# Weight sums in the first eight steps of gate and up, and the first output tile prepared from slot 114 of attention on

## The chip, the cores and the metric

The kernel runs on one core of a Trainium2 chip. The metric is the device time of one execution in microseconds (us); 2352.47 is the median of three runs before the change (2349.41 to 2353.89). Engines: PE is TensorE (matmuls; PEld its weight loads), DVE is VectorE, ACT is ScalarE, POOL is GpSimd, SP is SyncE, which here issues every DMA in one queue, in order.

## The reference

The reference is one transformer block on 4096 tokens of 512 features: linear attention with 16 query heads on 4 key heads, a residual and a layer norm, then a feed-forward part whose inputs go through a Hadamard transform, a second residual and a layer norm.

```python
q, k, v = x @ Wq.T, x @ Wk.T, x @ Wv.T            # 16, 4 and 4 heads of 128
q, k = rope(q), rope(k)
qf, kf = elu(q) + 1, elu(k) + 1
state_t = state_(t-1) + kf_t (outer) v_t;  z_t = z_(t-1) + kf_t
out_t = (qf_t @ state_t) / (qf_t . z_t + 1e-6)
x = layernorm(x + out @ Wo.T)
h = fwht(x * SU_ug) / 64
h = silu(h @ W_gate.T * (Wscale * 64)) * (h @ W_up.T * (Wscale * 64))
h = fwht(h * SU_dp) / 64
x = layernorm(x + h @ W_down.T * (Wscale_dp * 64))
```

## The kernel before

Every matmul operand is split into a high and a low part (`hilo`, lines 92 to 94: a copy on ACT, then a subtraction on DVE or POOL), and each product is three matmuls (high x high, high x low, low x high).

**Attention.** Tokens come in 16 blocks of 256, and the loop runs over them twice, once for key heads 0 and 1 and once for 2 and 3: 32 blocks n of four slots (g, p), 128 slots i, `NQ = 128`. A slot projects a pair of query heads (`proj_q`, L279), makes scores (`scores`, L372 and L373, then the sum of their halves on DVE, L382 and L383, and a causal mask on POOL, L386) and applies them (`av`, L406 and L407). `av` writes the numerators to `num_d` and the denominators to `den_d` in DRAM, for each tile t of 128 tokens. `recip(b)` (L123) loads the denominators of a block, inverts them and writes `rec_d`; it is called for a block of the second pass after its last slot, one block later (L571).

Beside this the loop loads and splits the second pass's weights (slots 54 to 58), splits the 16 heads of Wo and puts both parts into `wo_d` (`wo_stage`, at slots 112 to 116), loads them back as the storage of used weights comes free (`wo_fetch`), and forms weight sums for gate and up (`wcomb`, in blocks 18 to 25). `wcomb(p)` loads four quarter matrices A11, A12, A21, A22 from `wug` and makes S3 = A11 - A21, S1 = A21 + A22, S2 = S3 - A22, S4 = A12 + S2 on POOL (L429), each put into `was_d`.

A scheduler orders the instructions of each engine, so the place in the source is not the place in the queue: it may pull such side work many slots forward. In the order of the built kernel the sums stand in blocks 14 to 19, and the Wo splits in blocks 19 to 22.

**Output projection.** 32 tiles t. `pre(t)` loads the numerators (`nt`, 1 MB) and the residual (`yp`); `pre_rb` loads a row of reciprocals, spread over all partitions (`rb`, 256 KB, one for each key head g). `norm_o` (L708) multiplies them (g even on DVE, L713; g odd on POOL, L716) and splits the product; `wo_tile` (L157) runs 48 matmuls a tile into `ps_wo`. The first tile is made at the end of attention (lines 574 to 585, `ps_w0`): its `pre(0)` stands at slot 124, where the storage of the attention's inputs (`early`) is closed and that of `late["p"]` opens in its place. Layer norm, the transforms (`front`) and the preparation of the down weights (`prep_down`) run beside it.

**Gate and up.** 32 steps n = (f, p): 4 stretches of tokens by 8 pairs of weight tiles, each a product of two by two blocks in seven multiplications (Winograd's form; SEQ, WKEY). In step n, `asplit(n + 1, s)` splits the operands of the next step, and `aload(n + 2, s, ...)` loads those of the one after: three or four from `wug`, the sums from `was_d`, into `rp` (10 buffers). The results of a step are multiplied and summed on POOL (L900, L978) and put into `hop_d` one step later (`late_puts`).

**Down projection.** 56 units of 48 matmuls (L1041), with the second residual and layer norm; it isn't touched.

Of the kernel before, what the change touches and what calls it, by code (L numbers as in the profile page):

```python
# [9 lines left out]
F32 = mybir.dt.float32  # L10
# [33 lines left out]
def kernel(  # L44
# [8 lines left out]
    def dma(dst, src, pin=False):  # L53
        if dst.dtype == F32R:
            dst = dst.bitcast(F32)
        if src.dtype == F32R:
            src = src.bitcast(F32)
        i = nc.sync.dma_start(dst, src)  # L58
        if pin:
            tc.keep_in_program_order(i)  # L60
# [46 lines left out]
        dma(wo_d[h][0], hi)  # L107
        dma(wo_d[h][1], lo)

    def wo_fetch(h0, h1):  # L110
        for h in range(h0, h1):
            if h < NH - 2:
                hi, lo = (wres.tile([128, 512], F32R, tag="w", name=x) for x in ("wh", "wl"))
            else:
                w = late["p"].tile([128, 2, 512], F32R, tag="wx", name="wx")
                hi, lo = w[:, 0], w[:, 1]
            dma(hi, wo_d[h][0])
            dma(lo, wo_d[h][1])
            WO.append((hi, lo))

    late = {}

    def recip(b):  # L123
        dn = pout.tile([128, 2, 16], F32, tag="dn", name="dn", bufs=2)
        for j in range(2):
            dma(dn[:, j], den_d[2 * b + j].rearrange("g h c q -> (g h c q)").rearrange("(p n) -> p n", p=128))
        V.reciprocal(dn, dn)
        for j in range(2):
            dma(rec_d[2 * b + j].rearrange("(p n) -> p n", p=128), dn[:, j])

    cur = {}

    def pre_rb(t, g, pin=False):
        rb = late["p"].tile([128, 512], F32, tag="rb", name="rb", bufs=4)
        dma(rb, rec_d[t][g * 512:(g + 1) * 512].partition_broadcast(128), pin)
        cur[t]["rb"].append(rb)

    def pre(t):
        if t in (12, 16):
            recip(NB - 2 + (t == 16))  # L140
        nt = late["p"].tile([128, 16, 128], F32, tag="nt", name="nt", bufs=2)
        cur[t] = dict(nt=nt, rb=[])
        if t:
            dma(nt, num_d[t].rearrange("p g n -> p (g n)"), t < 3)
        if t < 2:
            for g in range(4):
                if t == 0:
                    dma(nt[:, 4 * g:4 * g + 4], num_d[t][:, g])
                pre_rb(t, g, t == 1 and g == 0)
        if t % 2 == 0:  # L150
            k = t // 2 % 3
            cur["yp"] = (late["c2"].tile([128, 2, DM], F32, tag="yp", name="yp", bufs=1) if k == 2 else
                         late["p"].tile([128, 2, DM], F32, tag="yp", name="yp", bufs=2))
        cur[t]["yp"] = cur["yp"]
        dma(cur["yp"][:, t % 2], x_n[t * 128:(t + 1) * 128])

    def wo_tile(t, ps, after=None):  # L157
        i = 0
        for g in range(KVH):
            oh, ol = cur[t][g]  # L160
            for h in range(4):
                wh, wl = WO[4 * g + h]
                for l, r in ((oh, wh), (oh, wl), (ol, wh)):
                    T.matmul(ps, l[:, h], r, start=i == 0, stop=i == 47)  # L164
                    i += 1
            if after is not None:
                after(g)


    with ExitStack() as es:  # L170
# [246 lines left out]
                    dma(den_d[2 * b + j][gg].rearrange("h c q -> c h q"),  # L417
                        ds[2 * j:2 * j + 2].rearrange("c (h q) -> c h q", h=4))

        def wcomb(p):  # L420
            r = {}
            for it in range(2):
                for kh in range(2):
                    x = wres.tile([128, 2, 2, 128], F32, tag="w", name="wq")
                    dma(x, wug[2 * p + it].rearrange("p (u k m) -> p u k m", u=2, k=4)[:, :, 2 * kh:2 * kh + 2])
                    r[it, kh] = x
            for key, o, a, b, op in (("S3", (0, 0), (0, 0), (1, 0), ALU.subtract), ("S1", (1, 0), (1, 0), (1, 1), ALU.add),
                                     ("S2", (1, 1), (0, 0), (1, 1), ALU.subtract), ("S4", (0, 1), (0, 1), (1, 1), ALU.add)):
                G.tensor_tensor(r[o], r[a], r[b], op)  # L429
                dma(was_d[p][key], r[o].rearrange("p u k m -> p (u k m)"))  # L430

        N = 2 * NB
        slots = [(n, g, p) for n in range(N) for g in range(2) for p in range(2)]
# [58 lines left out]
        for i, (n, g, p) in enumerate(slots):  # L492
# [8 lines left out]
                weights_q(1, 0)  # L501
            if r == 3 - QA:
                weights_q(1, 1)
            if 4 * 28 <= i < 4 * 28 + 4:
                for h in range(3 * (i - 112), 3 * (i - 112) + 3):
                    wo_stage(h)
            if i == 4 * 29:
                for h in range(12, 16):
                    wo_stage(h)
            if i == NQ - 10:  # L510
                wo_fetch(0, 2)
            if i == NQ - 6:
                wo_fetch(2, 6)
            if i == NQ - 5:
                wo_fetch(6, 10)
            if i == NQ - 4:
                wo_fetch(10, 14)
                early.close()
                late["s"] = ExitStack()
                late["p"] = late["s"].enter_context(tc.tile_pool(name="cl", bufs=2, side="right", reuse_waits="tile"))  # L520
                pre(0)
                wo_fetch(14, 16)
            go(gq)
            if sl == (0, 1):
                go(gk)
            if sl == (1, 0):
                go(gk)
            gq2 = proj_q(i + QA) if i + QA < NQ else None
            go(gq2)
            if sl == (0, 0):  # L530
# [33 lines left out]
            for x in gsc:  # L564
                go(x)
            gq = gq2
            if sl == (1, 0) and 18 <= n < 26:
                wcomb(n - 18)
            if sl == (1, 1):
                if NB + LAG <= n < N - 2 + LAG:  # L570
                    recip(n - NB - LAG)  # L571
                blk.pop(n - 1, None)

        pre(1)
        for x in range(2):
            o2 = [p3.tile([128, 2, 4, 128], F32R, tag=t, name=t, bufs=4) for t in ("qh", "ql")]
            for y in range(2):
                g = 2 * x + y
                rb = cur[0]["rb"][g].rearrange("p (h n) -> p h n", h=4)
                (G if y else V).tensor_tensor(rb, cur[0]["nt"][:, 4 * g:4 * g + 4], rb, ALU.mult)  # L580
                hilo(o2[0][:, y], o2[1][:, y], rb)
                cur[0][g] = (o2[0][:, y], o2[1][:, y])
        ps0 = pmm.tile([128, DM], F32, tag="mm", name="ps_w0")
        wo_tile(0, ps0)
        V.tensor_tensor(cur[0]["yp"][:, 0], ps0, cur[0]["yp"][:, 0], ALU.add)
# [100 lines left out]

    def aload(n, s, x):
        p, key = n % 8, WKEY[s]
        if key[0] == "A":
            it, kh = 2 * p + (key[1] == "2"), key[2] == "2"  # L690
            dma(x, wug[it].rearrange("p (u k m) -> p u k m", u=2, k=4)[:, :, 2 * kh:2 * kh + 2])
        else:
            dma(x, was_d[p][key].rearrange("p (u k m) -> p u k m", u=2, k=2))
        RAW[n, s] = x

    def asplit(n, s):
        hi, lo = (wres.tile([128, 2, 2, 128], F32R, tag="w", name=x) for x in ("woh", "wol"))
# [4 lines left out]
    with ExitStack() as es:  # L702
# [4 lines left out]

        def norm_o(t, g):  # L708
            c = cur[t]
            rb = c["rb"][g].rearrange("p (h n) -> p h n", h=4)  # L710
            if g % 2 == 0:
                o32 = pon.tile([128, 4, 128], F32, tag="on", name="ps_on")
                V.tensor_tensor(o32, c["nt"][:, 4 * g:4 * g + 4], rb, ALU.mult)  # L713
            else:
                o32 = p2.tile([128, 4, 128], F32, tag="o32", name="o32")
                G.tensor_tensor(o32, c["nt"][:, 4 * g:4 * g + 4], rb, ALU.mult)  # L716
            hi, lo = (p2.tile([128, 4, 128], F32R, tag="o", name=n, bufs=8) for n in ("oh", "ol"))
            hilo(hi, lo, o32)
            c[g] = (hi, lo)
# [65 lines left out]
        for t in range(32):  # L785
            if t + 2 < 32:
                pre(t + 2)
            def after(g):
                if t == 31:
                    for s in (2 * g, 2 * g + 1):  # L790
                        if s < 7:
                            asplit(0, s)
                if t + 1 < 32:
                    norm_o(t + 1, g)
                    if t + 2 < 32:
                        pre_rb(t + 2, g)

            yp = cur[t]["yp"]
            if t:
# [67 lines left out]
    with ExitStack() as es:  # L867
# [23 lines left out]
        for n in range(NS):  # L891
# [3 lines left out]
            def emit(u, q, x):  # L895
# [3 lines left out]
                else:  # L899
                    G.tensor_tensor(x, x, c.pop(("g", q)), ALU.mult)  # L900
                    c["h", q] = x

            if n in (1, 2, 4, 5):
                step(fr, 9)
                fr = ff_front(12 + (1, 2, 4, 5).index(n))
            new = {}
            for s, tag in enumerate(SEQ):
# [3 lines left out]
                for u in (1, 0):  # L911
# [20 lines left out]
                    if s == 5:  # L932
                        if u == 1:
                            x = utile("sg")
                            S.activation(x, ps, AF.Silu, scale=sc)
                            c["g", 2] = x
                        else:
                            x = c.pop(("g", 2))
                            V.scalar_tensor_tensor(x, ps, sc, x, ALU.mult, ALU.mult)
                            c["h", 2] = x  # L940
                if n and s in (1, 2, 3):
                    for _ in range(3):
                        if late_puts:
                            late_puts.pop(0)()
# [175 lines left out]
```

## Time and profile before

| what | us |
|---|---|
| median of three runs | 2352.47 |
| the profiled execution | 2353.87 |
| its span, first to last instruction | 2352.2 |
| attention, up to the first ps_wo | 0 to 976.1 |
| output projection | 976.1 to 1366.7 |
| gate and up | 1366.7 to about 2010 |
| down projection | about 2011.7 to 2352.2 |

The mean granted clock of TensorE was 0.990. PE was busy for 97% of the span, but a busy PE counts the overlap of pipelined matmuls, so a stage is judged by the idle time between them and by the time that a block, tile or step takes. The DMA queue moved 500.94 MB, 213 GB/s on average, with stretches above 280.

In the profile's rows a group of instructions is given as line, engine, operation, output <- inputs, shapes, count, then busy us and mean ns, then the idle time of that engine just before and what ended it. A row of waits gives who waited for whom, us in total, how often, and the longest. The chain of waits is followed back from the last instruction: start us, length, what.

### The profile page before, as it was taken

The numbers are of one execution on the slowest core, as the hardware profiler recorded it, in microseconds if no ns is written. First come the engines' busy times: TensorE is split into PE (matmuls) and PEld (weight loads), VectorE is DVE, ScalarE is ACT, GpSimd is POOL, SyncE is SP. The second block draws the span as 40 slices with busy tenths as digits, with TensorE's granted clock in tenths as the row PEclk, the third lists the DMA queues.
The fourth block names the chain that finished last, engine by engine and source line by source line (L and its number), as shares of the span: only waits on it lengthen the run. The fifth ranks groups of instructions, "written<-read, shape, count | busy, mean of one in ns | idle before, by whom it ended". The sixth has DMA issues, their size and how long they took to land.

```text
span 2352.2 us, 42395 instructions
## 1 busy us (share of the span) xinstructions
PE 2272.5 (97%) x14432; PEld 2013.3 (86%) x14432; DVE 1804.5 (77%) x2794; ACT 1401.9 (60%) x2482; POOL 1256.5 (53%) x1005
## 2 busy tenths in 40 slices
PE   8999999998899999899999999999999999899998
PEld 8999999887889999688878777788878888799998
DVE  8999999888898888578888775676776766665555
ACT  7777777766677777344434365655655655555553
POOL 4545544567655444358776626565565556633332
PEclk9999999999999999899999999999999999999999
DMA  6555555676785446879889976775665756877673
GB/s 205 169 162 147 148 149 153 192 223 202 236 268 147 134 139 201 286 252 284 250 277 271 280 255 196 246 252 188 225 210 188 243 188 197 265 248 249 225 250 118
DMA packets 378744, 500.94 MB, mean 213 GB/s; under 512 B 69694, under 2 KB 225408, under 8 KB 374560
## 3 DMA queue, kind: packets, MB, share of 16 engines
q1 hardware_dynamic: 378528, 498.24, 68.0%
q8 instruction: 114, 1.87, 0.3%
q14 instruction: 102, 0.84, 0.1%
HBM read 291.15 MB, written 165.15 MB: 194 GB/s over the span
## 4 chain that ended last, share of the span: by engine, by line
PE 74%; DVE 9%; DMA 7%; issue 4%; POOL 3%; ACT 2%; SPq 1%; DVEq 0%; ACTq 0%; POOLq 0%
PE ps_a L918 14%; PE ps_wo L164 13%; PE ps_qk L279 11%; PE ps_da L1041 7%; PE ps_b L918 7%; PE ps_num L406 4%; PE ps_db L1041 4%; PE ps_c L918 4%; PE ps_s L329 3%; PE ps_v L232 2%; PE ps_dc L1041 2%; DMA rb<-rec_d 1%; DVE x L265 1%; SPq L58 1%; PE ps_sc L372 1%
## 5 line engine op out<-in xcount | busy, mean ns | idle before, releaser
L386 POOL TENSOR_SCALAR_AFFINE_SELECT A<-A 64x512 fp32r<-64x512 f32 x256 | 224.6, 878 | 294.1 <-DVE am L382 195.7
L279 PE MATMUL ps_qk<-xh,wh 128*128 128x256 f32 x1280 | 358.8, 280 | 4.2 <-DVE x L265 4.1
L279 PE MATMUL ps_qk<-xh,wl 128*128 128x256 f32 x1280 | 356.5, 279 | 0.0
L279 PE MATMUL ps_qk<-xl,wh 128*128 128x256 f32 x1280 | 356.4, 278 | 0.0
L94 DVE TENSOR_TENSOR wol<-A,woh 128x512 fp32r<-128x512 f32 x217 | 226.5, 1048 | 113.7 <-ACT woh L93 97.1
L900 POOL TENSOR_TENSOR cc<-cc 128x512 f32<-128x512 f32 x96 | 149.7, 1561 | 292.3 <-ACT cc L897 156.7
L261 POOL TENSOR_TENSOR sw<-sw,csb 128x512 f32<-128x512 f32 x160 | 220.8, 1381 | 111.2 <-ACT sw L260 96.9
L279 PEld LDWEIGHTS ps_qk<-xh,wh 128*128 128x128 f32 x1280 | 241.9, 189 | 6.3 <-DVE x L265 4.9
L279 PEld LDWEIGHTS ps_qk<-xl,wh 128*128 128x128 f32 x1280 | 241.5, 189 | 1.1
L279 PEld LDWEIGHTS ps_qk<-xh,wl 128*128 128x128 f32 x1280 | 241.2, 188 | 0.8
L93 ACT ACTIVATE woh<-A 128x512 fp32r<-128x512 f32 x217 | 135.6, 630 | 136.6 <-PE ps_b L918 78.9
L93 ACT ACTIVATE hah<-hraw 128x512 fp32r<-128x512 f32 x224 | 139.2, 630 | 130.0 <-PE ps_da L1041 62.5
L918 PE MATMUL ps_a<-yoh,woh 128*128 128x512 f32 x512 | 202.8, 397 | 5.8 <-DVE yp L802 3.6
L94 POOL TENSOR_TENSOR hal<-hraw,hah 128x512 fp32r<-128x512 f32 x80 | 108.0, 1353 | 185.0 <-PE ps_da L1041 60.2
L918 PE MATMUL ps_a<-yol,woh 128*128 128x512 f32 x512 | 203.0, 397 | 0.0
L918 PE MATMUL ps_a<-yoh,wol 128*128 128x512 f32 x512 | 200.1, 397 | 0.0
L94 DVE TENSOR_TENSOR hal<-hraw,hah 128x512 fp32r<-128x512 f32 x144 | 107.3, 754 | 115.2 <-PE ps_da L1041 41.9
L164 PE MATMUL ps_wo<-wh,oh 128*128 128x512 f32 x434 | 174.5, 402 | 4.8 <-ACT oh L93 4.8
L164 PE MATMUL ps_wo<-wh,ol 128*128 128x512 f32 x434 | 173.6, 400 | 0.0
L164 PE MATMUL ps_wo<-wl,oh 128*128 128x512 f32 x434 | 173.4, 400 | 0.0
L266 ACT ACTIVATE sw<-x,neg 128x512 f32<-128x512 f32 x160 | 115.4, 721 | 82.0 <-DVE x L265 81.0
L925 ACT ACTIVATE sv<-ps_a,wsc 128x512 f32<-128x512 f32 x192 | 127.3, 680 | 42.2 <-PE ps_a L918 42.2
(228 smaller groups left out, 7289.0 us busy)
## 6 DMA issues: line engine op xcount, KB each, us to landing
hraw<-hop_d SPq DMA_DIRECT2D x224, 256.0 KB
vd<-vhl SPq DMA_DIRECT2D x128, 256.0 KB
num_d<-num SPq DMA_DIRECT2D x128, 256.0 KB
rb<-rec_d SPq DMA_DIRECT2D x128, 256.0 KB
hop_d<-hS SPq DMA_DIRECT2D x128, 256.0 KB
nt<-num_d SPq DMA_DIRECT2D x31, 1024.0 KB
A<-in_wug_dram SPq DMA_DIRECT2D x93, 256.0 KB
hop_d<-cc SPq DMA_DIRECT2D x64, 256.0 KB
```

Source lines behind the costliest of these rows:

```text
L93: S.activation(hi, src, AF.Copy)
L94: eng.tensor_tensor(lo, src, hi.bitcast(F32), ALU.subtract)
L164: T.matmul(ps, l[:, h], r, start=i == 0, stop=i == 47)
L261: G.tensor_tensor(sw, sw, sinb, ALU.mult)
L266: S.activation(sw, x1, AF.Exp, bias=neg1)
L279: T.matmul(ps[:, j], W[key][wa][:, k * 128:(k + 1) * 128], B[xa][:, k], start=i == 0, stop=i == 11)
L386: G.affine_select(ah, ah.bitcast(F32), pattern=[[0, 8], [1, 64]], compare_op=ALU.is_ge, fill=0.0, base=0, channel_multiplier=-1)
L406: T.matmul(ps[:, c2], l, r, start=i == 0, stop=i == len(ops) - 1)
L900: G.tensor_tensor(x, x, c.pop(("g", q)), ALU.mult)
L918: T.matmul(ps, w[:, u, k], y[:, k], start=first and i == 0, stop=i == 5, skip_group_check=not first)
L925: S.activation(x, ps, AF.Copy, scale=sc)
L1041: T.matmul(ps[:, j], ops[qd][al][:, r, js], BW[s][bl][ip], start=first and i == 0, stop=i >= 45, skip_group_check=True)
```

## The change

- `wcomb` is gone from attention. For n < 8, `aload` loads A11, A12, A22 and, into the place of S1, A21. `asums(p)` makes the four sums in those buffers, two on DVE and two on POOL, and returns the four stores into `was_d`, which are issued from the fifth unit (s > 3) of a step on. It is called for p = 0 in the last tile of the output projection and for p = n + 1 at the start of step n < 7. From n = 8 on, the sums come from `was_d` as before.
- `wo_stage` is done for 12 heads instead of 16, from slot 94 on, one a slot. The last four heads are loaded raw at slot 125 and split there (`wo_raw`, `wo_split`).
- The first tile: for key heads 0 and 1, `nt` and `rb` are loaded from slots 114 and 116 on, multiplied on POOL and split; for 2 and 3 from slot 125 on. Before, all four began at slot 124.
- `recip` is cut in two: `recip_load` after a block, the inversion half a block later; for the last two blocks the load comes two tiles earlier.
- `rb` has 3 buffers instead of 4 and is loaded 7 quarters of a tile ahead (8 before); `yp` has 2 buffers in one pool and 1 in the other, the other way round than before.

```diff
+    def wo_raw(hs):
+        raw = late["p"].tile([128, 4, 512], F32, tag="nt", name="woraw", bufs=2)
+        for k, h in enumerate(hs):
+            w = late["p"].tile([128, 2, 512], F32R, tag="wx", name="wx", bufs=4)
+            dma(raw[:, k], wo[h])
+            WO.append((w[:, 0], w[:, 1], raw[:, k]))
+
+    def wo_split(eng, *hs):
+        for h in hs:
+            hilo(*WO[h], eng)
...
+    def pre_rb(k):
+        if k < 128:
+            RB[k] = late["p"].tile([128, 512], F32, tag="rb", name="rb", bufs=3)
+            dma(RB[k], rec_d[k // 4][k % 4 * 512:k % 4 * 512 + 512].partition_broadcast(128), k < 7)
...
+        if t in (10, 14):
+            cur["dn"] = recip_load(NB - 2 + (t == 14))
         if t in (12, 16):
-            recip(NB - 2 + (t == 16))
+            recip(*cur["dn"])
...
+        def o_load(g, hi, lo):
+            nt = praw.tile([128, 512], F32, tag="raw", name="nt0")
+            dma(nt, num_d[0][:, g])
...
+        def o_mul(g):
+            G.tensor_tensor(O0[g][3], O0[g][2], O0[g][3], ALU.mult)
...
-            if 4 * 28 <= i < 4 * 28 + 4:
-                for h in range(3 * (i - 112), 3 * (i - 112) + 3):
-                    wo_stage(h)
-            if i == 4 * 29:
-                for h in range(12, 16):
-                    wo_stage(h)
-            if i == NQ - 10:
-                wo_fetch(0, 2)
+            if NQ - 34 <= i < NQ - 22:
+                wo_stage(i - NQ + 34)
+            if i == NQ - 14:
+                o_load(0, *(wres.tile([128, 4, 128], F32R, tag="w", name=x) for x in ("oh0", "ol0")))
+            if i == NQ - 13:
+                o_mul(0)
+            if i == NQ - 12:
+                o_load(1, *(wres.tile([128, 4, 128], F32R, tag="w", name=x) for x in ("oh0", "ol0")))
+                o_split(0, G)
+            if i == NQ - 11:
+                o_mul(1)
+            if i == NQ - 9:
+                o_split(1, G)
...
+            if i == NQ - 3:
                 early.close()
...
+                for y in range(2):
+                    o_load(2 + y, o2[0][:, y], o2[1][:, y])
+                pre_rb(4)
+                wo_raw(range(12, 16))
+                pre_yp(0)
+                pre(1)
+            if i == NQ - 2:
+                o_mul(2)
+                o_mul(3)
+            if i == NQ - 1:
+                wo_split(G, 12, 13)
...
-            if sl == (1, 0) and 18 <= n < 26:
-                wcomb(n - 18)
...
+        o_split(2, V)
+        pre_rb(5)
+        o_split(3, V)
+        pre_rb(6)
+        wo_split(V, 14)
+        wo_split(G, 15)
         ps0 = pmm.tile([128, DM], F32, tag="mm", name="ps_w0")
...
+        RAW[n, s] = x
+        if n < 8:
+            key = {"S1": "A21"}.get(key, key)
...
+    def asums(p):
+        r = {WKEY[s]: RAW[p, s] for s in range(7)}
+        V.tensor_tensor(r["S3"], r["A11"], r["S1"], ALU.subtract)
+        G.tensor_tensor(r["S2"], r["S3"], r["A22"], ALU.subtract)
+        G.tensor_tensor(r["S1"], r["S1"], r["A22"], ALU.add)
+        V.tensor_tensor(r["S4"], r["A12"], r["S2"], ALU.add)
+        return [lambda k=k: dma(was_d[p][k].rearrange("p (u k m) -> p u k m", u=2, k=2), r[k])
+                for k in ("S3", "S2", "S1", "S4")]
...
+            if t == 31:
+                sum_puts = asums(0)
...
                 if t + 1 < 32:
                     norm_o(t + 1, g)
-                    if t + 2 < 32:
-                        pre_rb(t + 2, g)
+                    pre_rb(4 * t + g + 7)
...
+            if n < 7:
+                sum_puts += asums(n + 1)
...
+                if s > 3:
+                    for _ in range(3):
+                        if sum_puts:
+                            sum_puts.pop(0)()
```

## The prediction

> **What bounds the kernel now.** First the engines' shares and PE's windows: PE is the bound nearly everywhere, so a change pays only where PE isn't dense. A block is one n of the attention loop (four slots); its start is the first num eviction (L410) of the block in ScalarE's timeline: block 14 at 445.1, 16 at 513.9, 19 at 606.6, 23 at 733.9, 30 at 928.3. The windows below are cut there (PE, PEld, DVE, ACT, POOL busy us, granted clock, DMA share, GB/s).
>
> ```profile
> PE 2272.5 (97%) x14432; PEld 2013.3 (86%) x14432; DVE 1804.5 (77%) x2794; ACT 1401.9 (60%) x2482; POOL 1256.5 (53%) x1005
> ...
> core 0: us, PE busy (x) PEld busy (x) DVE busy (x) ACT busy (x) POOL busy (x), PEclk, DMA share, GB/s
> 445.10:513.90 68.80, 62.34 (x478) 58.12 (x478) 60.34 (x97) 43.32 (x78) 47.22 (x41) 0.98 0.73 216
> 513.90:606.60 92.70, 82.20 (x638) 76.50 (x638) 75.14 (x115) 56.49 (x102) 61.37 (x54) 0.98 0.70 214
> 606.60:733.90 127.30, 116.86 (x913) 107.50 (x912) 112.75 (x177) 89.12 (x161) 75.27 (x64) 1.00 0.77 236
> 733.90:928.30 194.40, 194.40 (x1589) 185.60 (x1588) 170.44 (x299) 142.90 (x253) 91.95 (x91) 1.00 0.52 148
> 928.30:976.10 47.80, 36.20 (x209) 29.62 (x207) 27.88 (x47) 18.02 (x34) 17.20 (x18) 0.89 0.83 261
> 976.10:1366.70 390.60, 383.02 (x1664) 307.19 (x1665) 313.23 (x499) 169.26 (x342) 265.21 (x202) 0.98 0.87 271
> 1366.70:1523.50 156.80, 152.90 (x661) 121.87 (x662) 100.01 (x140) 98.72 (x182) 83.51 (x64) 0.99 0.73 230
> ```
>
> Blocks 23 to 29 are PE-dense: 194.4/7 = 27.8 us a block. Blocks 14-15 lose 68.8 - 55.6 = 13.2, blocks 16-18 92.7 - 83.4 = 9.3, blocks 19-22 127.3 - 111.2 = 16.1 us, and the turn from attention to the output projection (928.3 to 976.1) holds 11.6 us of idle PE at a clock of 0.89. Then who PE waited for in 445 to 734, and what ran there beside the usual work (groups of POOL in 514 to 607 and in 607 to 734):
>
> ```profile
> PE ps_num L406 <- POOL A L386: 11.6, 13, 2.7
> PE ps_sc L372 <- DVE A L383: 10.2, 11, 2.2
> ...
> L429 POOL TENSOR_TENSOR wq<-wq 128x512 f32<-128x512 f32 x16 | 23.0, 1439 | 16.2 <-DMA wq<-in_wug_dram 12.2 <-issue 3.7
> ...
> L94 POOL TENSOR_TENSOR wl<-raw,wh 128x512 fp32r<-128x512 f32 x8 | 12.0, 1504 | 6.4 <-ACT wh L93 6.4
> ```
>
> PE waits for the masks on POOL and the score sums on DVE while POOL makes weight sums (L429) or Wo splits (L94). Last the chain of waits through the turn, and SP's waits:
>
> ```profile
> 941.51 6.52 DMA rb<-rec_d
> 948.15 0.69 DVE rb L580
> ...
> 953.05 4.63 PE ps_w L164 x10
> ...
> 968.66 5.90 DMA rb<-rec_d
> 974.69 0.71 DVE ps_on L713
> ...
> SPq L58 <- POOL o L716: 55.4, 30, 6.8
> SPq L58 <- DVE ps_on L713: 28.3, 19, 4.6
> ```
>
> Twice PE's path runs through an rb load: 6.5 us for the first output tile, 5.9 for the second.
>
> **The change part by part.** Places are those in the order of the built kernels, counted by blocks.
>
> *Weight sums out of attention.* Removed: 32 sums of 1.43 us on POOL (blocks 14 to 19) with 32 loads and 32 stores of 0.26 MB (16.8 MB). The built order also moves the Wo splits: 12 of 16 (a load, a copy on ACT, a subtraction on DVE or POOL, two stores each) go from blocks 19-22 into blocks 14-15. So blocks 16 to 22 keep only the usual 13 POOL instructions and 24 DMAs a block, but for block 17 with 4 POOL, 2 ACT and 7 DMA more (first tile, heads 0 and 1; 4 x 1.4 us of POOL, which idles 53% of a dense block). At the dense rate: 7 x 27.8 = 194.6 against 220.0 measured: **-25.4**. Cover: PE itself; if DMAs of block 15 spill over, it is the 5 us below.
>
> *Blocks 14-15.* They lose 8 sums and gain 12 Wo splits. Bytes by the order: 19.8 MB against 14.7; at 280 GB/s (about the best windows) 70.7 us against 68.8 now: +2. DVE has 115 instructions against 96; 60.3 us busy for 97 is 0.62 each: 60.3 + 19 x 0.62 = 72, +3. By the loss in blocks 19-22, 16.1/16 = 1.0 us a split: 13.2 - 8 x 9.3/18 + 12 = 21.1 against 13.2: +8. A spill into block 16 adds up to 5. I take **+7**, nearest the row of the same work; ends +2 and +13. In return PE has done some 72 matmuls of projections ahead, which leave the turn.
>
> *The turn.* Before 976.1 the order now has 129 matmuls at 0.117 us start to start (24 of L279 in 2.8) and 48 of the first tile at 0.233 (12 of L918 in 2.8): 26.3 us of PE, against 36.2. Half of the first tile's operands are there since block 17, so 24 of its matmuls fill gaps. The rest: projections end 72 x 0.117 = 8.4 us earlier, so the storage opens and rb for heads 2 and 3 is issued about 5 us after block 30's start (941.5 - 928.3 = 13.2 now), lands 6.5 later, at 11.5. POOL then has 2 products and 3 splits at 1.35 and 12 masks at 0.82, 16.6 us: masks done at 28, last num at 29.5 (38.2 now): -8.7. Added here: 4 raw Wo loads, 4 ACT copies, 3 POOL splits and one DVE split in place of 8 loads; queued behind the POOL splits are the masks of the last slots, for which PE waits; that is in the 16.6. Behind the first tile's addition, DVE keeps the last four slots' sums (8 x 0.69), also in it. Then rb: the second tile's first part (rb 4) is early, but rb 5 stands on SP behind the last den stores, as all four do now. Issue 2.2 after the last num, 5.9 landing, 1.3 POOL, 0.6 ACT, while 2.9 us of matmuls run: the second part starts 10 us after the last num, against 12.4 now: -2.4. Sum **-11**. Ends: PE-bound with a fast landing, 26.3 + 4.4 against 47.8, -17; rb no earlier than now and the splits on top, 0. The 24 Wo loads stand denser (block 29 holds 8.7 MB against 5.5: 31 us at 280 GB/s, 3 us late); what they delay is that same rb.
>
> *Output projection.* rb has 3 buffers instead of 4. A tile takes 390.6/31 = 12.6 us, a quarter 3.15: lead 9.45 instead of 12.6. The landings that the chain shows are 5.9 to 6.7, the product 0.88 or 1.30: 7 to 8 us, so the ring turns in time, but SP already waits on these products (83.7 us above). **+3**; ends -4 (the rb waits of now) and +20. Reciprocals are split from their loads: 1.2 us of DVE a block, hidden under dense PE. yp's buffers change places only: nothing, under tiles loaded two ahead; without that cover, a landing a tile.
>
> *Gate and up.* Steps 0 to 7 get 16 sums on POOL (1.43: 22.9 us) and 16 on DVE (0.69 to 1.05: 11 to 17), 32 stores, and lose 24 loads. In 1366.7 to 1523.5 (eight steps) POOL idles 73 us and DVE 57. New waits: the fourth sum holds DVE until POOL has made the second; behind it stand evictions and splits, for which PE waits. SP's stores wait for sums with the next step's loads behind; now these loads go out some 40 us ahead (step 3's at 1382.6 to 1388, its start 1366.7 + 3 x 19.6), which hides it. Two sums fall in 1350 to 1366, where DVE is full before the first matmul: +1.4. **+2**; ends -3 and +30 (rival two).
>
> The splits' own row shows what POOL's company costs DVE:
>
> ```profile
> L94 DVE TENSOR_TENSOR wol<-A,woh x56: 679/692/1825, 1375.7 to 1520.6; 128x512 fp32r<-128x512 f32 x56
> ```
>
> Median 0.69, longest 1.83. The Trainium skill (SBUF — State Buffer, Who interferes with whom) says that a DVE instruction with two SBUF inputs and a GpSimd instruction that reads SBUF exclude each other for a whole instruction. By the rule each POOL sum may stop a split for 1.43 us: 16 x 1.43 = 23 us, an estimate, in full on the path +23; by the rows it falls into DVE's 57 idle us and costs nothing.
>
> **Sum.** -25.4 + 7 - 11 + 3 + 2 = -24.4. Against the profiled run's 2353.87 (span 2352.2 and 1.7 around it): 2329.5. The median shown, 2352.47, lies 1.4 lower: **2328**.
>
> **Rivals.** *One, the ring of three rb buffers becomes the bound (slower).* For: DMA share 0.87 in that stage, SP waits on rb's readers. Against: the shown landings leave 1.4 us. If load, product and SP's queue take 10.5 us on average, a quarter takes 3.5 instead of 3.15: 124 x 0.35 = 43; 2353.9 - 27.4 + 43 = 2369, 2368 on the median's scale. The gain is gone from 27.4/124 = 0.22, a turn of 10.1 us.
>
> *Two, sums stall gate and up.* The second sum behind POOL's queue (h sums and product, 2.88 + 1.63 + 1.30 + 1.29 = 7.1 us at 1397) holds DVE; one unit of matmuls (2.8) covers: 4.3 x 7 = 30, so 2328 - 2 + 30 = 2356. Against: POOL and DVE are half idle.
>
> *Three, the moved Wo splits and the turn eat most.* Blocks 14-16 at +13, the turn at 0: -25.4 + 13 + 3 + 2 = -7.4: 2345. For: 19.8 MB in two blocks; against: block 16 is light (3.2 MB).
>
> *That the change doesn't take effect* is excluded for POOL: in the built order no sum stands in attention.
>
> **How the numbers follow.** Forecast 0.62, one 0.12, two 0.12, three 0.14. A difference of 0.2% (4.7 us) is about what can be told from none. Faster: 0.62 + 0.10 of three + 0.02 of two = 0.74; same: 0.04 + 0.03 + 0.03 = 0.10; slower: 0.09 of one + 0.07 of two = 0.16. The range begins at the forecast's low end and leaves out most of one and two, some 0.2. The forecast's own range is 2312 (turn -17, blocks +2, projection and gate 0) to 2340 (blocks +13, gate and projection 6 more). Up to 2351 it takes in three and the mild ends of the others.
>
> **What would show it.** Right: 27.8 us a block from 16 to 22; blocks 14-15 at 71 to 76 us with DMA share above 0.9; the first ps_wo some 31 us after block 30's start, then one gap before its second part; no PE waits for sums in gate and up. Wrong: PE waiting for oh all along the projection (one), DVE idle before line 734's sums (two), blocks 16-17 over 29 us or rb landing at 20 us in the turn (three).

## The result and the profile after

The changed kernel takes 2382.65 us (median of four runs, 2379.57 to 2389.35) beside 2351.9 for before: a ratio of 1.0135, 95% interval 1.0109 to 1.0161. It is slower by some 31 us, where 24 less were forecast. The profiled execution took 2384.97 us, its span is 2383.2 (before: 2353.87 and 2352.2), so the two traces can be compared stage by stage.

Marks that both traces have: ScalarE's first num eviction of a block, VectorE's yp addition that ends an output tile, the last sg of gate and up, the end of ScalarE's last instruction. Durations between them in us, each from one profiled execution; e5, e10 and e12 are experiments below:

| stage | before | forecast | after | difference | e5 | e12 | e10 |
|---|---|---|---|---|---|---|---|
| blocks 14-15 | 68.8 | +7 | 71.4 | +2.6 | 72.7 | 70.3 | 68.7 |
| blocks 16-22 | 220.0 | -25.4 | 214.9 | -5.1 | 186.7 | 186.9 | 211.9 |
| blocks 23-29 | 194.4 | 0 | 207.6 | +13.2 | 195.6 | 195.7 | 194.2 |
| turn (block 30 to tile 1) | 62.0 | -11 | 53.0 | -9.0 | 54.9 | 54.3 | 63.1 |
| output projection (tile 1 to 31) | 375.6 | +3 | 390.0 | +14.4 | 377.1 | 375.9 | 375.7 |
| gate and up (to the last sg) | 642.4 | +2 | 656.3 | +13.9 | 654.9 | 647.9 | 641.7 |
| down projection | 340.4 | 0 | 340.7 | +0.3 | 340.0 | 339.4 | 341.2 |

The profiled executions lie up to 6 us from the medians of their kernels (e10 6.1 above, e1 5.4 and e12 5.1 below), so a difference of a few us between the stages of two kernels settles little by itself.

The windows of after, cut at its own marks (block 14, 16, 19, 23, 30, first ps_wo, first ps_a, ninth sg); columns as in the prediction's windows:

```profile
core 0: us, PE busy (x) PEld busy (x) DVE busy (x) ACT busy (x) POOL busy (x), PEclk, DMA share, GB/s
446.20:517.60 71.40, 67.06 (x509) 63.18 (x510) 66.67 (x108) 52.21 (x95) 41.22 (x35) 0.95 0.87 266
517.60:614.60 97.00, 88.87 (x679) 83.38 (x678) 77.21 (x129) 62.19 (x112) 46.69 (x43) 0.95 0.52 134
614.60:732.50 117.90, 114.49 (x920) 109.11 (x919) 96.05 (x169) 80.42 (x145) 56.74 (x52) 0.99 0.46 127
732.50:940.10 207.60, 197.66 (x1560) 187.58 (x1559) 165.20 (x292) 138.45 (x250) 97.46 (x91) 0.97 0.52 145
940.10:973.10 33.00, 28.15 (x159) 23.10 (x158) 19.56 (x31) 13.17 (x27) 17.64 (x19) 0.95 0.66 231
973.10:1383.80 410.70, 388.75 (x1665) 304.87 (x1665) 314.67 (x502) 166.59 (x342) 266.57 (x204) 0.99 0.83 259
1383.80:1588.60 204.80, 191.29 (x803) 151.74 (x804) 154.94 (x185) 122.85 (x221) 129.33 (x91) 0.96 0.71 234
```

POOL and the DMA queues are lighter in blocks 16 to 22, as meant (POOL 103.4 us against 136.6). But PE isn't dense there, and not in blocks 23 to 29 either, where before it was: 9.9 us of idle PE and a clock of 0.97. The first row below says who PE waits for in blocks 14 to 29, the others who VectorE waits for from block 19 on (us in total, times, longest):

```profile
PE ps_sc L381 <- DVE A L392: 18.6, 12, 3.9
```

```profile
DVE dn L137 <- DMA dn<-den_d: 30.3, 10, 4.0
DVE x L274 <- POOL sw L270: 15.9, 11, 1.5
...
DVE dn L137 <- issue: 4.2, 1, 4.2
```

The first line of VectorE is new: in before's blocks 19 to 29 this wait is 2.1 us in two times (and 4.4 in six for which the profile shows no releaser). Two more of these waits, 10.2 us, stand in after's blocks 17 and 18. One of the ten in VectorE's timeline, and another in the chain of waits (start, us, what):

```profile
821.41 0.67 DVE L391 TENSOR_TENSOR am<-ps_sc,A 64x512 f32<-64x512 f32 x1
825.18 0.35 DVE L137 RECIPROCAL dn<-dn 128x32 f32<-128x32 f32 x1 [3.10 <-DMA dn<-den_d]
825.45 0.63 DVE L278 SCALAR_TENSOR_TENSOR sw<-sw,x 128x512 f32<-128x512 f32 x1
826.11 0.69 DVE L392 TENSOR_TENSOR A<-ps_sc,am 64x512 fp32r<-64x512 f32 x1
```

```profile
758.26 4.00 DMA den_d<-ds
...
762.32 3.76 DMA dn<-den_d
...
766.34 0.13 DVE dn L137
...
766.61 0.64 DVE sw L278
...
767.27 0.70 DVE A L392
...
768.02 0.38 PE ps_sc L381
```

The reciprocal takes 0.35 us, but it stands between the two halves of a score (am, A), and VectorE takes its instructions in order. So A, and behind it PE's next score (ps_sc), wait for a round trip through DRAM: denominators stored (4.00), loaded again (3.76). All 13 reciprocals of after's blocks 17 to 29 stand so. From block 17 on PE waits ten times for A by more than 0.2 us, 16.1 us in all, and each of these waits ends 1.7 us after the start of a reciprocal for which VectorE had stood 2.9 to 5.3 us.

In before's order the reciprocal stood, six times of ten, behind VectorE's work on the next block's keys (dz). There VectorE could wait, too, while PE stayed dense:

```profile
786.13 0.73 DVE L303 TENSOR_REDUCE dz<-kft 128x4 f32<-128x256 f32 x2
788.89 0.35 DVE L127 RECIPROCAL dn<-dn 128x32 f32<-128x32 f32 x1 [2.02 <-issue]
789.16 0.67 DVE L262 TENSOR_TENSOR ps_qk<-ps_qk,csb 128x512 f32<-128x512 f32 x1
```

In the output projection VectorE waits for rb (before: 8.3 us in 7 times):

```profile
DVE ps_on L755 <- DMA rb<-rec_d: 62.7, 31, 7.0
```

In gate and up the largest gap of PE, 6.2 us at 1422.3, is a wait for an eviction; before has no wait of this kind. PE's row up to the ninth sg, and VectorE's timeline ahead of the gap's end:

```profile
PE ps_c L964 <- DVE cc L976: 8.3, 2, 6.2
```

```profile
1415.95 1.75 DVE L94 TENSOR_TENSOR wol<-A,woh 128x512 fp32r<-128x512 f32 x1
1417.62 1.78 DVE L734 TENSOR_TENSOR A<-A 128x512 f32<-128x512 f32 x1
1419.32 3.48 DVE L94 TENSOR_TENSOR wol<-A,woh 128x512 fp32r<-128x512 f32 x2
1423.38 1.09 DVE L731 TENSOR_TENSOR A<-A 128x512 f32<-128x512 f32 x1 [0.58 <-DMA A<-in_wug_dram]
1424.40 3.41 DVE L94 TENSOR_TENSOR wol<-A,woh 128x512 fp32r<-128x512 f32 x2
1427.73 1.40 DVE L976 SCALAR_TENSOR_TENSOR cc<-ps_c,wsc,sv 128x512 f32<-128x512 f32 x2
```

The evictions of ps_c (cc) come after sums (L731, L734) and splits (L94) for later steps, and all of these but one take about 1.7 us instead of 0.69; POOL is busy beside them (6.3 of the 6.5 us from 1422.0 on, windows at the end).

### The profile page after: what moved, and what is told of

It is laid out like the page before. It is cut to its first block, busy times and chain, and to the rows that moved or that the text cites. A ratio compares the mean times of both kernels' runs of the same rounds, so it can differ in the third digit from the quotient of the medians.

```text
span 2383.2 us, 42198 instructions
## 1 busy us (share of the span) xinstructions
PE 2287.9 (96%) x14432; PEld 2022.9 (85%) x14432; DVE 1802.3 (76%) x2805; ACT 1397.3 (59%) x2482; POOL 1244.8 (52%) x994
## 4 chain that ended last, share of the span: by engine, by line
PE 66%; DMA 13%; DVE 11%; issue 4%; POOL 3%; ACT 2%; SPq 1%; DVEq 0%; ACTq 0%; POOLq 0%
PE ps_a L964 14%; PE ps_qk L288 10%; PE ps_da L1091 8%; PE ps_b L964 7%; PE ps_wo L173 5%; DMA rb<-rec_d 5%; PE ps_num L415 4%; PE ps_db L1091 4%; PE ps_c L964 4%; PE ps_s L338 2%; PE ps_v L241 2%; DMA den_d<-ds 2%; PE ps_dc L1091 2%; DMA dn<-den_d 1%; DVE x L274 1%
## 5 line engine op out<-in xcount | busy, mean ns | idle before, releaser
L395 POOL TENSOR_SCALAR_AFFINE_SELECT A<-A 64x512 fp32r<-64x512 f32 x256 | 231.9, 906 | 356.7 <-DVE am L391 203.5
L94 DVE TENSOR_TENSOR wol<-A,woh 128x512 fp32r<-128x512 f32 x217 | 228.5, 1059 | 122.5 <-ACT woh L93 90.7
L94 POOL TENSOR_TENSOR hal<-hraw,hah 128x512 fp32r<-128x512 f32 x80 | 106.7, 1336 | 185.3 <-PE ps_da L1091 63.8
L94 DVE TENSOR_TENSOR hal<-hraw,hah 128x512 fp32r<-128x512 f32 x144 | 105.3, 740 | 117.3 <-PE ps_da L1091 37.5
L173 PE MATMUL ps_wo<-wh,oh 128*128 128x512 f32 x372 | 149.6, 402 | 3.3 <-ACT oh L93 3.3
L173 PE MATMUL ps_wo<-wh,ol 128*128 128x512 f32 x372 | 149.3, 401 | 2.1 <-DVE ol L94 2.1
L173 PE MATMUL ps_wo<-wl,oh 128*128 128x512 f32 x372 | 148.1, 398 | 0.0
```

Of the source, the lines that this page charges most:

```text
L94: eng.tensor_tensor(lo, src, hi.bitcast(F32), ALU.subtract)
L395: G.affine_select(ah, ah.bitcast(F32), pattern=[[0, 8], [1, 64]], compare_op=ALU.is_ge, fill=0.0, base=0, channel_multiplier=-1)
```

## The experiments

**e1: the split of the reciprocal undone in the text.**

```diff
-                if "dn" in cur:
-                    recip(*cur.pop("dn"))
...
-                    cur["dn"] = recip_load(n - NB - LAG)
+                    recip(*recip_load(n - NB - LAG))
```

> After, with the reciprocal again called together with its load at the end of a block, as before. The order of the built kernel hardly moves by it: on VectorE the reciprocal still stands between the two halves of a score (am and A). Theory 'the order': the loss in attention is made by the place that the reciprocal has in VectorE's order, which came with the new order of the whole steady block, not by the split in the text; then 2383 within 5 us, and VectorE still stands some 3 us per block for dn. Rival 'the split': the loss comes from splitting load and reciprocal; then 2355 to 2363, 20 to 28 us less.

Measured: 2382.12 us (2376.73 to 2386.11), 1.014 of before (1.0115 to 1.0166); VectorE's wait for dn from block 19 to 29 is 33.6 us in 11 times. The split in the text is not the cause.

**e2: the reciprocal one slot later.**

```diff
-        V.reciprocal(dn, dn)
+        i = V.reciprocal(dn, dn)
+        if pin:
+            tc.keep_in_program_order(i)
...
-                if "dn" in cur:
-                    recip(*cur.pop("dn"))
...
+                if "dn" in cur:
+                    recip(*cur.pop("dn"), True)
```

(The call stands at the end of the next block's last slot, before the next load; keep_in_program_order puts it behind all that VectorE was given until then.)

> After, with the reciprocal held behind the second half of the next slot's score, about eight VectorE instructions (some 6 us) later than in after; all else stays. Theory 'VectorE stands for dn inside a score': the 3 us stands of 10 to 14 blocks are gone, blocks 17 to 29 take 28 us instead of 29.4, block 30 starts 14 to 22 us earlier, total 2361 to 2369. Rival 'late vd and DMAs, the stand is only where lateness shows': PE's waits move to another tile and the total stays within 5 us of 2383.

Measured: 2352.46 us (2350.64 to 2354.73), 1.0004 of before (0.9994 to 1.0013): 30 us less than after, more than expected. VectorE's timeline and the windows of blocks 14-15, 16-18, 19-22 and 23-29:

```profile
782.30 0.69 DVE L394 TENSOR_TENSOR A<-ps_sc,am 64x512 fp32r<-64x512 f32 x1
783.03 0.35 DVE L137 RECIPROCAL dn<-dn 128x32 f32<-128x32 f32 x1
```

```profile
445.00:517.30 72.30, 65.41 (x509) 60.49 (x510) 69.25 (x108) 52.53 (x95) 40.56 (x35) 1.00 0.86 263
517.30:594.40 77.10, 76.88 (x627) 73.31 (x626) 69.78 (x119) 56.11 (x101) 38.59 (x37) 1.00 0.44 122
594.40:704.00 109.60, 109.13 (x884) 103.47 (x884) 94.45 (x161) 79.53 (x142) 59.86 (x56) 1.00 0.55 149
704.00:899.60 195.60, 195.60 (x1599) 186.80 (x1598) 168.13 (x295) 141.33 (x251) 90.60 (x91) 1.00 0.52 148
```

(In the built order a number of VectorE's other instructions trade places with a neighbour.) The reciprocal waits for nothing in these blocks now, PE is dense from block 16 on, and block 30 starts at 899.6 instead of 940.1. Of these 40 us the turn takes back 6.2 (59.2 against 53.0), as e2 has 49 matmuls of the last block in the turn that after had done before it, and the projection 3.9 (393.9 against 390.0). My size was wrong because I counted the stands alone. Over blocks 14 to 29 after has 18.2 us more of idle PE than e2 (25.8 against 7.6, windows above), and its PE is also busy 21.1 us longer (468.1 against 447.0) for 49 more matmuls, which are worth about 6 (447.0/3619 each): some 15 us are matmuls at a lower clock.

**e3: a fourth rb buffer.**

```diff
-            RB[k] = late["p"].tile([128, 512], F32, tag="rb", name="rb", bufs=3)
+            RB[k] = (late["c2"].tile([128, 512], F32, tag="rb3", name="rb", bufs=1) if k % 4 == 3 and k > 3 else
+                     late["p"].tile([128, 512], F32, tag="rb", name="rb", bufs=3))
...
+        pre_rb(7)
...
-                    pre_rb(4 * t + g + 7)
+                    pre_rb(4 * t + g + 8)
```

> After, with a fourth rb buffer (from the pool of the output projection) and rb loaded eight quarters ahead, as before. Theory 'ring': of the 14.5 us that the output projection lost between its tiles 1 and 31, 10 to 14 come back and VectorE's wait for rb falls from 59 us to about 8: total 2369 to 2373. Rival 'the raw Wo splits and the moved yp buffers, or a DMA queue that is behind anyway, make it': less than 4 us comes back, total 2379 to 2387.

Measured: 2367.96 us (2367.1 to 2368.17), 1.0074 (1.0058 to 1.009). The projection takes 378.3 us from tile 1 to 31 (after 390.0), and the wait is down to a third:

```profile
DVE ps_on L756 <- DMA rb<-rec_d: 21.0, 9, 4.0
```

The ring made 11.7 of the 14.4. (The later kernels with four buffers take 375.0 to 381.2 there; before took 375.6.)

**e4: the weight sums in attention again.**

```diff
+            if sl == (1, 0) and 18 <= n < 26:
+                wcomb(n - 18)
...
-                sum_puts = asums(0)
...
-                sum_puts += asums(n + 1)
```

(wcomb and the loads of all sums in aload are those of before.)

> After, with the weight sums formed in attention again (POOL, blocks 18 to 25 of the text), all other parts of the change kept. Theory: gate and up returns to its time before (14 us less) and the built order of the steady block returns to that of before, where the reciprocal stands behind work that waits for nothing; attention comes to before's 928 at block 30 (12 us less), the turn's -9 and the projection's +14 stay: 2353.9 - 9 + 14 = 2357 to 2361. Rival 'the sums in gate and up cost little, the lateness there is handed on from the projection': 2366 to 2372, gate and up still 10 us longer than before.

Measured: 2363.84 us (2362.79 to 2367.22), 1.006 (1.0042 to 1.0077), some us above the theory's range. Block 30 starts at 927.8 (before 928.3), and gate and up takes 642.1 us (before 642.4): both as the theory has it. VectorE's built order around the reciprocal is for the most part again that of before (seven of eleven stand behind dz), though the call is still split. The projection keeps its loss (389.8, with the ring of three). The turn is where the theory failed: it takes 61.1 us, 0.9 less than before and not 9, though its part of the change is kept, and the 49 matmuls that after had done ahead are back in it.

**e5: e2 and e3 together.**

> The reciprocal held one slot later (e2) and the fourth rb buffer (e3) together, all else as in after. If the two losses are separate terms they add: 2352.5 (e2) less 14.4 (what e3 took off after) = 2336 to 2341, faster than before by 0.5 to 0.7%; from the first sg of gate and up to the last, still 11 to 14 us more than before. Rival 'one lateness, handed on': what the one repair gains the other has already had, 2346 to 2353.

Measured: 2333.18 us (2332.3 to 2333.95), 0.9914 (0.9899 to 0.9929): the two terms add, with 3 us more than expected, and the change is faster than before. Gate and up still takes 12.5 us more than before. The next four are about that. (Kernels with the same code in this stage, after, e1, e2, e3 and e5, take 654.0 to 657.2 us in it.)

**e6, e7, e8: three ways of sums in gate and up.** e6 has all four sums on POOL:

```diff
-        V.tensor_tensor(r["S3"], r["A11"], r["S1"], ALU.subtract)
+        G.tensor_tensor(r["S3"], r["A11"], r["S1"], ALU.subtract)
...
-        V.tensor_tensor(r["S4"], r["A12"], r["S2"], ALU.add)
+        G.tensor_tensor(r["S4"], r["A12"], r["S2"], ALU.add)
```

> As e5, with all four weight sums of a step on POOL instead of two on VectorE and two on POOL. Theory 'VectorE's queue': two sums ahead of evictions and splits make PE wait in gate and up; without them 6 to 12 of its 14 us come back, 2326 to 2333. Rival 'late loads': SP's stores of sums stand before the next steps' loads and hold their buffers; POOL forms the sums later still, nothing comes back or up to 6 us are lost, 2336 to 2345.

e7 makes asums a generator with a yield after the second sum, two after the third and one after the fourth, ahead of the stores, and steps it once a matmul group:

```diff
-                sum_puts += asums(n + 1)
+                sums = asums(n + 1)
...
+                if n < 7:
+                    step(sums)
```

> As e5, with the four sums of a step called one after the other between its seven matmul groups (the first two in the first, the third in the second, the fourth in the fourth) and the four stores together after it. Theory 'VectorE's queue': as the sums no longer stand in one heap before the evictions, 3 to 8 us come back, 2330 to 2336. Rival 'late loads': the stores come no earlier, so within 3 us of e5.

e8 leaves the stores out, and steps from 8 on load as many bytes of a weight tile where they would load a sum, so they compute with other weights:

```diff
-            dma(x, was_d[p][key].rearrange("p (u k m) -> p u k m", u=2, k=2))
+            dma(x, wug[2 * p].rearrange("p (u k m) -> p u k m", u=2, k=4)[:, :, 0:2])
...
-                            sum_puts.pop(0)()
+                            sum_puts.pop(0)
```

> As e5, but the sums are formed and not stored: the 32 stores of weight sums are left out, and steps 8 to 31 load a quarter of the first weight tile where they would load a stored sum (the same bytes), so later steps compute with other weights. Theory 'late loads' (stores on SP's queue and the buffers that they hold delay the next A loads): gate and up comes to its time before, 10 to 14 us less than e5, 2324 to 2329. Rival 'VectorE's queue': less than 4 us, 2333 to 2340.

| | median us | ratio to before | gate and up, against before's 642.4 |
|---|---|---|---|
| e6 | 2332.34 | 0.9908 (0.9893 to 0.9923) | +12.3 |
| e7 | 2338.08 | 0.9931 (0.9911 to 0.9951) | +16.6 |
| e8 | 2334.98 | 0.9924 (0.9906 to 0.9941) | +11.2 |

The stores and the late loads are not it: without any store 11.2 of 12.5 stay. Nor does it help to take the sums off VectorE: e6's median lies in the range of the theory 'VectorE's queue', but its interval overlaps e5's, and in the stage nothing came back. With the sums spread (e7) the median lies above what both its theory and its rival had. e6 shows a part of the reason. Its timeline of VectorE, and two rows of POOL, which makes sums and products without a pause meanwhile:

```profile
1361.86 11.91 DVE L94 TENSOR_TENSOR wol<-A,woh 128x512 fp32r<-128x512 f32 x7
```

```profile
1364.75 1.75 POOL L735 TENSOR_TENSOR A<-A 128x512 f32<-128x512 f32 x1
1366.45 1.71 POOL L736 TENSOR_TENSOR A<-A 128x512 f32<-128x512 f32 x1
```

Seven splits take 1.70 us each; the median in before was 0.69. From the last output tile to the ninth sg, 8.6 of the 20.8 us that VectorE's sums took in e5 came back as longer splits (68 of them, 78.5 us against 69.9). The rest did leave VectorE, and yet the stage is no shorter.

**e9: all sums on VectorE.**

```diff
-        G.tensor_tensor(r["S2"], r["S3"], r["A22"], ALU.subtract)
-        G.tensor_tensor(r["S1"], r["S1"], r["A22"], ALU.add)
+        V.tensor_tensor(r["S2"], r["S3"], r["A22"], ALU.subtract)
+        V.tensor_tensor(r["S1"], r["S1"], r["A22"], ALU.add)
```

> As e5, with all four weight sums on VectorE and none on POOL. Theory 'sharing': in e6 seven splits on VectorE beside POOL's sums took 1.70 us each instead of 0.69, in e5 VectorE's own sums 1.49 on average (20.8 for 14); with POOL out of it a sum takes 0.69, VectorE's busy time from the last output tile to sg 8 falls from 164 to about 160 us though it makes twice as many sums, the sums no longer wait for POOL, and 3 to 8 us come back: 2325 to 2331. Rival 'VectorE has no room': 14 more instructions on VectorE cost more than POOL's company, 2333 to 2342.

Measured: 2329.97 us (2325.98 to 2330.9), 0.9903 (0.9887 to 0.992); gate and up +9.4. The time lies in the theory's range, but its interval overlaps that of e5, so the total alone settles nothing. Within the stage 3 of 12.5 us came back. The durations of VectorE's instructions from the last output tile to the ninth sg, added up, did not fall to 160 as expected (168 us, e5 164): its 28 sums took 30.7, 1.10 each, beside POOL's remaining products. So sharing is real, but to take POOL's sums away gives back only a small part of the loss.

**e10: before, with the reciprocal held as in e2.** The edit is that of e2, on the kernel before, with the inversion split from its load as in the change.

> Before, with the reciprocal split from its load and held one slot later, as in e2; nothing else of the change. Theory: before's reciprocal stood behind work that waits for nothing (4.4 us of waits in all), so the place is worth nothing there: within 4 us of before, 2348 to 2356, and the 40 us of e2 repair what the change had made. Rival 'a late reciprocal is a gain of its own': 8 us or more faster than before, and then that much of e2's gain isn't owed to the removed sums.

Measured: 2340.99 us (2339.71 to 2347.08), 0.9954 (0.9937 to 0.997). The theory fails here: 8 us gained in blocks 16 to 22, all of it in blocks 19 to 22 (117.9 against 127.3), where the Wo splits and before's last four sums run. The wait for dn is too small for it: before has 2.1 us of it in blocks 19 to 22 and 6.5 up to block 29, e10 none. Why the order that came with the held reciprocal is better there stays open, and so does how much of e2's 40 us is owed to such an order and not to the stands. What the change is worth in blocks 16 to 22 is then e5 against e10, both with a held reciprocal and with nearly the same matmuls (1506 and 1510): 186.7 against 211.9, 25.2 less. It is not the sums alone: e10 has 16 Wo splits in blocks 19 to 22, e5 none.

**e11: the sums back in attention, beside dense PE.**

```diff
+                tc.keep_in_program_order(G.tensor_tensor(r[o], r[a], r[b], op))
...
+            if 19 <= n < 27:
+                if sl == (0, 0):
+                    gw = wcomb(n - 19)
+                    go(gw)
+                if g == 1:
+                    go(gw)
+                    go(gw)
```

(wcomb makes one sum at a step; gate and up loads stored sums as before; the Wo splits are called 30 slots earlier in the text, so that they keep their place in blocks 14 and 15.)

> As e5, with the weight sums in attention again, but held in POOL's program order: two at each of the last two slots of blocks 19 to 26 of the text (20 to 27 of the order), where PE is dense and POOL idles half of the time; the Wo splits keep to blocks 14 and 15. Gate and up loads all stored sums, as before. Theory: a sum beside dense PE only delays masks, at most 1 us for each of 32 in the losses of before's blocks 19 to 22, and gate and up gives back 11: 2322 to 2335, the best of all kernels if the sums are hidden. Rival 'a sum in attention costs its full 1.43 us wherever it stands': 2333 - 11 + 46 = 2368.

Measured: 2329.56 us (2324.8 to 2331.05), 0.9897 (0.9881 to 0.9912). Gate and up is 2.5 us shorter than before's, so the sums are all of its loss. In attention, from block 19 to 30, e11 takes 320.6 us and e5 305.3: 15.3 for 32 sums, 0.48 each, neither hidden nor the rival's full price. e5 pays 15.0 for them in gate and up (12.5 and 2.5): the sums cost about the same in either place (e12's arrangement pays 8.0).

**e12: e9, with the sums of a step held behind the evictions of its second group.** The sums are called after the second group (s == 1), with the first of them kept in program order:

```diff
-                sum_puts += asums(n + 1)
+                AR = {WKEY[s]: RAW[n + 1, s] for s in range(7)}
...
+                if s == 1 and n < 7:
+                    sum_puts += asums(n + 1, AR)
```

> As e9 (all four sums on VectorE), with the sums of a step held in VectorE's order behind the evictions of the second matmul group of the step before, so that VectorE can't run ahead with the sums and splits of later steps while evictions wait. Theory 'order on VectorE' (evictions stand behind sums and splits for steps that are not due): of the 9.3 us that e9 still loses between the last output tile and sg 8, 4 to 9 come back, PE's idle gaps before ps_c go away: 2321 to 2326. Rival 'VectorE's load': 14 more instructions in 8 steps cost what they cost in any order, or the held sums make the splits late: 2328 to 2338.

Measured: 2325.2 us (2320.13 to 2326.15), 0.9893 (0.9876 to 0.9909), the lowest median of all; the intervals of e9, e11 and e12 overlap. PE's gaps before ps_c (3.38 and 2.22 us in e9) are gone; others before ps_b, up to 2.04, have come. Gate and up is at +5.5 to its last sg, 4 less than e9, but by the ninth sg only 1.0 of e9's 9.3 has come back, where the theory had 4 to 9; the rest of the gain came later, where no sums run. So the total lies in the theory's range and the stage doesn't bear it out. That VectorE's order, and not its load, makes the loss is not shown, and e6 doesn't fit the load alone: this stays open.

## Why the prediction was wrong, step by step

Forecast and result lie some 55 us apart: some 33 of them in blocks 16 to 29, 11 in the output projection and 12 in gate and up.

*Weight sums out of attention (-25.4 for blocks 16 to 22): 25.2 less between e10 and e5; but -5.1 in after.* That 25.2 meets 25.4 is in part luck: both ends lie 8 us below mine (211.9 against 220.0, 186.7 against 194.6). The step that failed is one that I put at nothing in another paragraph: "Reciprocals are split from their loads: 1.2 us of DVE a block, hidden under dense PE". I asked how long VectorE is taken (the instruction itself has 0.35 us) and not what stands behind it at its place in VectorE's order. Without the sums the built order of the whole steady block is another one, and in it the reciprocal stands inside a score and VectorE waits there for 1.6 to 5.3 us each time. e1 shows that the split of the text has no part in this, e4 that the order comes back with the sums, e2 that another place, with the order that came with it, is worth 40 us in after up to block 30. It also undid my dense rate for blocks 23 to 29, which the change doesn't touch: +13.2 (e2 has 195.6). The order could be read before the run; I had used it to count instructions, not to ask what each new neighbour waits for.

*Blocks 14-15 (+7): +2.6 in after, +3.9 in e5*, near the bound by bytes (+2), so the row of bytes was the better one. My count was off, too: before's blocks 14 and 15 hold 12 of the sums, not 8, and blocks 16 to 18 hold 16, not 18; with these the third estimate gives +5 and not +8.

*The turn (-11): -9.0*, near, and in after by the way that I gave: 49 matmuls had left it (I had 72), the last num came 30.6 us after block 30's start (29.5 forecast), the first ps_wo 33.0 after it (31). But this held only in the order that cost 40 us before it. In e2 and e5 the 49 matmuls are back, the last num is about as late as in before (37.5 and 38.7, against 38.3), and the turn gains 2.8 and 7.1. What e5 gains stands behind the last num, where I had 2.4: the first ps_wo follows it by 2.4 us, 9.5 in before.

*Output projection (+3): +14.4.* This is rival one, at 14.4/120 = 0.12 us a quarter instead of its 0.35. I set a lead of 9.45 us against 7 to 8, from landings of 5.9 to 6.7. The landings in the changed kernel's chain of waits through this stage run from 3.6 to 9.0 us, four of 19 above 7; two of them:

```profile
1063.68 7.42 DMA rb<-rec_d
```

```profile
1102.21 8.96 DMA rb<-rec_d
```

A margin of 1.4 us between means isn't one when landings scatter. How much of it went to them and how much to SP's queue is not told apart here. The 2.7 us that e3 leaves are the most that yp's other pools and the raw Wo heads can have cost there.

*Gate and up (+2): +13.9.* Rival two named the place, not the cause: VectorE stands at the fourth sum once, for 1.3 us. The term that was mis-sized is the sums' cost on VectorE: it had 23 us more to do (154.9 against 132.0 up to the ninth sg, windows of equal marks), as its 14 sums in that stretch took 19.6 us, 1.40 each. By the rows I had taken 0.69 to 1.05 and let the idle time of a whole stage hide them; they and the splits of later steps stand ahead of evictions for which PE waits (8.3 us, above). Whether it is this order or the load that costs the time e12 leaves open. The Trainium skill (SBUF — State Buffer, Who interferes with whom) has the sharing that the durations here show, 1.70 against 0.69 us a split in e6. The estimate of +23 by that rule was nearer to 13.9 than my +2, though taking POOL's sums away (e9) gave back only 3.

## What to carry to other kernels

When work is taken out of a steady loop, the order of all that remains can change. On each in-order engine, look at what every waiting instruction stands in front of, above all loads that return through DRAM: here an instruction of 0.35 us, moved by one slot, gave back 40. Idle time averaged over a stage hides nothing by itself; cover counts only where the order puts it, and a ring of buffers needs a margin for the slowest landing, not the mean. Price a stall of PE at more than its length where, as after many gaps here, the matmuls behind it run slower.

## What was not expected of the hardware

The granted clock falls after short gaps too. The windows of after around two gaps, of 1.6 and 6.2 us:

```profile
619.50:621.10 1.60, 0.10 (x2) 0.06 (x1) 1.54 (x4) 0.91 (x2) 0.00 (x0) 1.00 0.08 7
621.10:625.00 3.90, 3.90 (x20) 3.48 (x21) 2.46 (x5) 1.71 (x3) 3.16 (x3) 0.66 0.01 1
...
1422.00:1428.50 6.50, 0.33 (x2) 0.00 (x0) 5.92 (x6) 1.21 (x2) 6.33 (x5) 0.69 0.94 321
1428.50:1434.00 5.50, 5.47 (x13) 4.31 (x14) 4.13 (x5) 1.64 (x3) 4.61 (x4) 0.50 1.01 361
```

After 1.6 us without work the clock (third column from the end) was 0.66 for 3.9 us, an estimated 3.9 x 0.34 = 1.3 us more; after 6.2 us it was 0.50 for 5.5 us, 2.7 more. But a gap of 3.4 us in e9 left it at full speed, while 3.3 us in after, up to 553.2, were followed by 0.64 over 4.8 us. The gap in e9:

```profile
1367.00:1370.60 3.60, 0.22 (x2) 0.04 (x1) 3.60 (x5) 0.68 (x2) 1.61 (x2) 1.00 0.96 339
1370.60:1375.00 4.40, 4.40 (x19) 3.58 (x20) 4.40 (x7) 1.84 (x3) 2.60 (x2) 1.00 1.04 367
```

The Trainium skill (TensorE: Matmul & The Clock Gate, HAM oscillation — how this bites in real kernels) asks for no idle gap over about 3.4 us; here a drop follows a gap of half that length, and of two gaps close to it one is followed by a drop and one is not, so the figure doesn't tell here which gap costs clock.

The drops themselves have a fixed size. In the records of after the clock is either full or at 0.50, each drop but the last of the kernel lasts 3.41 us or two or three times that, and their starts (554.11, 588.24, 622.37, 1424.50 among them) lie multiples of 3.41 us apart. The window around one of them:

```profile
618.95:622.37 3.42, 1.92 (x13) 1.38 (x11) 2.29 (x4) 1.74 (x3) 1.17 (x2) 1.00 0.06 7
622.37:625.78 3.41, 3.41 (x17) 3.23 (x17) 2.62 (x5) 1.93 (x6) 2.66 (x3) 0.50 0.00 0
625.78:629.20 3.42, 3.42 (x31) 3.42 (x31) 3.33 (x7) 2.22 (x5) 1.49 (x2) 1.00 0.27 97
```

17 matmuls stand where 31 follow at full clock, so a drop costs an estimated 1.7 us (3.41 x 0.5) for each 3.41 us that hold work. Which gaps bring a drop on may depend on where they fall between these points; no run here tests it.
